# A hybrid attention and feed-forward kernel on one core: ScalarE's order written out in the gated stage, and VectorE's in the feed-forward stages

## The chip, the cores and the metric

The kernel runs on one core of a Trainium2 chip. The time is that of the device, in microseconds (us), for one execution. PE is TensorE (PEld its weight loads), ACT ScalarE, DVE VectorE, POOL GpSimd, SP SyncE, which issues the transfers.

## What is computed

x is 2 sequences of 1024 tokens by 512 columns. Four stages follow one another, each with a layernorm ahead of it and its result added to x: a gated linear recurrence, a feed-forward net, a causal two-map attention, and the feed-forward net again. The weights of the net are made ternary first. The two parts that the change touches:

```python
# gated stage, 16 heads of 32 columns
q, k, v, a, g = split(layernorm(x) @ w_in.T, 5)
q = q * rsqrt(mean(q * q over the head) + RMS_EPS)
a = clip(sigmoid(a + 2.0), 0.6, 0.9995);  u = tanh(k) * v
prefix = cumprod(a over a chunk of 64 tokens)
mem[t] = a[t] * mem[t - 1] + u[t] * min(prefix / 1e-6, 1)
y = (q * mem) * sigmoid(g) + (1 - sigmoid(g)) * v
x = x + y @ w_out.T
# feed-forward: w = ternary(w), scale per 64 columns from mean(abs(w))
h = silu(layernorm(x) @ w_gate.T) * (layernorm(x) @ w_up.T)
x = x + (h @ w_proj.T) * rsqrt(mean(h * h) + RMS_EPS)
```

## The kernel before, in words

x stays on the chip as 16 tiles of 128 tokens by 512 columns. The gated stage works on 4 blocks of 512 tokens. All its matmuls are plain f32 and give columns on the partitions and tokens along the row.

**Start of a block.** `Input` (L284) holds the layernorm of four x tiles: statistics on DVE (L109, L110), the root on ACT (`rstd`, L112), the reciprocal and the scaling `xn` on DVE (L128), four transposes on PE (`xnt_a`, L137) and a copy on ACT (`a_xt`, L313). For block 0 this goes tile by tile; for a later block the statistics are made at once by the constructor, at the end of the block before the previous one, `normal` scales two of the tiles in c = 0 and 1 and two in c = 2, and `turn` transposes two in c = 2 and two in c = 3.

**Queries.** `queries` (L322) projects q by chunks of 128 columns, copies it (L337), squares it (`sq`, L339) and sums the squares by head with a matmul each into `pss` (L329), 128 columns of `headmean` wide of which 16 are in use. The last of these matmuls, the root over 16 partitions and the reciprocal stand in `roots` and `factors` (L351 to L359); `rq_parts` keeps the factor in two parts, and `pr` (a matmul with `headrow`) spreads it over a chunk's columns.

**A block** runs over c = 0 to 3, chunks of 128 columns. PE: `project(kv[:, 0])` is k, `project(kv[:, 1])` is v, then come the transposes for the next block, group means of the ternary weights (`pm`), then `project(ag[:, 0])` and `project(ag[:, 1])`, 4 matmuls of 512 columns each (L317). kv and ag are tiles of two banks of psum, one bank for each half, from one pool of two buffers. After all four projections, the code emits on ACT u = tanh(k), v, a = sigmoid and gate (L461 to L468); then DVE and POOL make the recurrence by two scans and the row yt. **End of a block:** the next block's queries, then 16 matmuls `a_out` (L529) and the addition to x (L534); after the first of them `roots`, after the second `factors`.

**Ternary weights** (`Ternary`, 16 chunks of 128 by 1536): ACT makes mag and sign (L193, L195), PE the group mean `pm` of each third, ACT the copy `scale` (L203), DVE six steps (L209 to L218), which `step` deals out between the other work; the seventh stores the chunk, calls `begin` (mag and sign) of the next and loads the one three ahead.

**Feed-forward** (from L571): for each of 4 blocks, 16 values of f. `gate_up` (L616 to L631): 8 + 8 matmuls, silu on ACT, the product h on DVE (L622), a copy on ACT (L624), hs on DVE (L625), squares on ACT and their sum on POOL. `down` (L637) comes one f later on PE, into `f_out`. The next block's statistics are made at f = 6, its `normal` one f ahead of its transposes. In the last block of the first net, `beside` calls `normal_stats` at f = 2 and `normalise` at f = 4 to 11 for the attention's first sequence; `normalise` emits the scaling (`xn_b`, L128) and the transposes (`xnt_b`, L137) together, and it is called after `gate_up` and ahead of `down`.

**What sets the order.** A tile framework places the instructions. Where a stage holds `manual_schedule` for an engine, that engine runs them as the code emits them; otherwise a scheduler orders them. In the gated stage PE and DVE were by hand (ACT only for block 0's input, L403), in the feed-forward stages PE and ACT, in the attention PE. Waits are put in by the framework, tile by tile:

```python
fixed = {mybir.EngineType.PE, mybir.EngineType.DVE}
order.enter_context(tc.manual_schedule(engines=fixed))
```

Of the kernel before, what the change touches and what calls it, by code (L numbers as in the profile page):

```python
# [17 lines left out]
P = 128  # L18
# [24 lines left out]
def kernel(  # L43
# [58 lines left out]

    def layernorm_begin(tiles, name, norm=norm):

        n = len(tiles)
        mv = norm.tile([P, n, 2], F32, tag="ln_mv", name=f"mv_{name}")
        for j, i in enumerate(tiles):
            st = norm.tile([P, 6], F32, tag="ln_st", name=f"st_{name}_{j}")
            nc.vector.bn_stats(st, xres[i])  # L109
            nc.vector.bn_aggr(mv[:, j, :], st)  # L110
        rstd = norm.tile([P, n], F32, tag="ln_rstd", name=f"rstd_{name}")
        nc.scalar.activation(rstd, mv[:, :, 1], AF.Sqrt, bias=ln_eps)  # L112
        return mv, rstd
# [107 lines left out]
    with ExitStack() as s:  # L221
# [38 lines left out]
        headmean = wa.tile([P, NKC, P], F32, name="headmean")  # L260
        nc.gpsimd.memset(headmean, 0.0)
        heads = headmean[:, :, :16]
        nc.gpsimd.memset(heads, 1.0 / HD)
        for base, sign in ((0, 1), (HD - 1, -1)):
            nc.gpsimd.affine_select(
                out=heads, in_=heads, compare_op=ALU.is_ge, fill=0.0, base=base,
                pattern=[[sign * P, NKC], [-sign * HD, 16]], channel_multiplier=sign,
            )
# [3 lines left out]
        for base in (0, 32):  # L272
            nc.gpsimd.affine_select(
                out=headrow, in_=headrow, compare_op=ALU.not_equal, fill=1.0, base=base,
                pattern=[[4, NKC], [1, 4], [0, HD]], channel_multiplier=-1,
            )

        rq_parts = []
        for i in range(2):
            z = wa.tile([P, BLK], F32R, name=f"rq_parts{i}")  # L280
            nc.vector.memset(z.bitcast(F32), 0.0)
            rq_parts.append(z)

        a_start = []  # L284
        for i in range(2):
            z = wa.tile([P, BLK], F32, name=f"a_start{i}")
            nc.vector.memset(z, 0.0)
            a_start.append(z)

        class Input:  # L290


            def __init__(self, t, at_once=True):
                self.tiles = range(t * TPB, (t + 1) * TPB)
                self.stats = layernorm_stats(self.tiles, f"a{t}") if at_once else None
                self.xt = xt_pool.tile([P, NKC, BLK], F32, tag="xt", name=f"a_xt{t}")
                self.xn, self.one = {}, {}
# [23 lines left out]
        def queries(t, xt, begun=None):  # L321


            q = ap_.tile([P, NKC, BLK], F32, tag="q", name=f"q{t}")
            pss = bank(f"pss{t}")
            late = []

            def mean_square(c, sq):
                nc.tensor.matmul(  # L329
                    pss, headmean[:, c, :], sq, start=(c == 0), stop=(c == NKC - 1)  # L330
                )

            for c in range(NKC):
                pq = begun if begun and not c else bank(f"pq{t}_{c}")
                if pq is not begun:
                    project(pq, w_q, c, xt)
                nc.scalar.copy(q[:, c, :], pq)  # L337
                sq = ap_.tile([P, BLK], F32, tag="sq", name=f"sq{t}_{c}")
                nc.scalar.square(sq, pq)  # L339
                if late:  # L340
                    mean_square(*late.pop())
                late.append((c, sq))
                if c < 3 and t:
                    quantise(c)
                elif c and not t:
                    quantise(c - 1)
            parts = rq_parts[t % 2]

            rq = ap_.tile([16, BLK], F32, tag="rq", name=f"rq{t}", bufs=1)

            def roots():  # L351
                mean_square(*late.pop())
                nc.scalar.activation(rq, pss[:16, :], AF.Sqrt, bias=rms_eps[:16])

            def factors():
                nc.vector.reciprocal(rq, rq)
                hi, lo = parts[:16], parts[32:48]
                nc.vector.tensor_copy(hi, rq)
                nc.vector.tensor_sub(lo, rq, hi.bitcast(F32))  # L359

            return q, parts, roots, factors
# [27 lines left out]
        fixed = {mybir.EngineType.PE, mybir.EngineType.DVE}  # L389
        order.enter_context(tc.manual_schedule(engines=fixed))  # L390
        before = [None] * NKC
        first = Input(0, at_once=False)
# [10 lines left out]
        with tc.manual_schedule(engines={mybir.EngineType.Activation}):  # L403
            for j in range(TPB + 1):
                if j < TPB:
                    first.measure(j)
                if j:
                    first.normal(j - 1)
                    first.turn(j - 1)
                if j == 3:  # L410
                    begin(0, 0)
# [8 lines left out]
        following = Input(1)  # L420
        for t in range(NBLK):
            yt = wa.tile([P, NKC, BLK], F32, tag="yt", name=f"yt{t}")
            last = t == NBLK - 1
            for c in range(NKC):
# [9 lines left out]
                project(kv[:, 0, :], w_k, c, xt)  # L434
                if t + c == 0:
                    roots()
                    factors()
                project(kv[:, 1, :], w_v, c, xt)
                if t + c == 0:
                    quantise(3)  # L440
                    step()
# [26 lines left out]
                nc.scalar.activation(gate, ag[:, 1, :], AF.Sigmoid)  # L468
# [5 lines left out]
                start = a_start[c % 2]  # L474
# [13 lines left out]
                if not last and c < 2:  # L488
                    following.normal(c)
# [36 lines left out]
            for j, k in products:  # L526
                if k == 0:
                    po[j] = bank(f"a_out{t}_{j}")
                nc.tensor.matmul(  # L529
                    po[j], yt[:, k, ts(j, P)], w_out[:, k, :], start=(k == 0), stop=(k == NKC - 1)  # L530
                )
                if k == NKC - 1:
                    xi = xres[t * TPB + j]
                    nc.vector.tensor_add(xi, xi, po[j])  # L534
                    if not last:
                        if j == 0:
                            roots()
                        elif j == 1:
                            factors()
                        for i in ((), (), (3, 0), (1, 2, 3))[j]:  # L540
                            quantise(i)
                            step()
            if not last:
                q, rq = q_next, rq_next
                following = Input(t + 2) if t + 2 < NBLK else None
# [13 lines left out]

    def normal_stats(b):  # L560
        stats[b] = layernorm_stats(range(b * NQ, (b + 1) * NQ), f"b{b}")
        xts[b] = edge_sb.tile([P, NKC, SEQ], F32, tag="xt", name=f"b_xt{b}")
# [11 lines left out]
    def feed_forward(which, store, first, beside=None):  # L574


        with ExitStack() as s:
# [82 lines left out]
            for f in range(NF):  # L660
# [3 lines left out]
                tc.manual_schedule(engines={mybir.EngineType.PE, mybir.EngineType.Activation})  # L664
# [10 lines left out]
            for t in range(NBLK):  # L675
# [5 lines left out]
                for f in range(NF):  # L681
# [28 lines left out]
        {2: lambda: normal_stats(0)}  # L710
        | {f: lambda j=f - 4: normalise(0, j, edge_bank) for f in range(4, 4 + NQ)},
# [564 lines left out]
```

## Time and profile before

| what | us |
|---|---|
| three runs: lowest, median, highest | 2138.49, 2139.43, 2142.36 |
| the profiled execution's span | 2138.4 |
| gated stage, 0 to 403: PE busy, DVE, ACT | 378.3, 289.4, 162.8 |
| first feed-forward, 403 to 765: PE, DVE, ACT | 361.8, 132.4, 144.0 |
| attention, 765 to 1773: PE, DVE, ACT | 1004.6, 540.0, 390.5 |
| second feed-forward, 1773 to the end: PE, DVE, ACT | 358.8, 121.9, 137.6 |
| granted TensorE clock, by stage | 0.98, 1.00, 1.00, 0.99 |

The span runs from the first to the last instruction that the profiler saw. The runs' times take in the little that lies around it. A busy time is the sum of an engine's instructions; the granted clock is TensorE's, as a share of full speed. In a line of the timeline the first number is the start, the second the time from the first start to the last end of a group of like instructions, and what stands in brackets is the idle time ahead of it and whose end it waited for. In the table of waits the numbers are the sum of the idle time, the number of waits and the longest.

### The profile page before, as it was taken

To read this page: it belongs to the slowest core of one execution; us is meant where nothing else is said; L and a number is where in the kernel's file an instruction comes from. 1 tells how busy PE (TensorE), PEld (TensorE's weight loads), DVE (VectorE), ACT (ScalarE), POOL (GpSimd) and SP (SyncE) were. 2 spreads that over 40 slices of the span, in tenths; PEclk is the share of its full clock that TensorE was granted. 3 is DMA by queue.
4 is the path that set the end of the run, shared out by engine and by line. 5 is a ranking of instruction groups with operands and counts; after the bars stand their busy time and mean duration, and the time that the engine had idled before them with its cause. 6 is when DMAs were issued, how large, how long until landed. Compare 5 with 4: busy or idle time off the path is not lost.

```text
span 2138.4 us, 28060 instructions
## 1 busy us (share of the span) xinstructions
PE 2103.5 (98%) x10632; PEld 1245.7 (58%) x10632; DVE 1083.6 (51%) x2282; ACT 834.9 (39%) x1589; POOL 462.3 (22%) x808
## 2 busy tenths in 40 slices
PE   8999999999999999999999999999999999999998
PEld 4444444588888854444444444444444447888887
DVE  5766768643344234555555465364646672433322
ACT  5343434244344322444444422243434433343433
POOL 1413223122222221211212113021212231121222
PEclk9999999999999999999999999999999999999999
DMA  7121111600000111101010101111110033000000
GB/s 264 66 89 59 59 59 59 250 1 1 1 1 1 35 47 37 41 22 45 21 46 21 46 8 37 38 32 34 31 36 16 14 114 133 8 13 20 1 21 20
DMA packets 51000, 98.71 MB, mean 46 GB/s; under 512 B 10801, under 2 KB 19121, under 8 KB 50865
## 3 DMA queue, kind: packets, MB, share of 16 engines
q1 hardware_dynamic: 50864, 96.93, 13.9%
q8 instruction: 83, 1.36, 0.3%
q14 instruction: 53, 0.43, 0.1%
HBM read 58.75 MB, written 16.78 MB: 35 GB/s over the span
## 4 chain that ended last, share of the span: by engine, by line
PE 89%; DVE 7%; ACT 2%; POOL 1%; DMA 1%; issue 1%; SPq 0%; DVEq 0%; ACTq 0%; POOLq 0%
PE y L995 13%; PE g L616 11%; PE u L616 11%; PE f_out L637 11%; PE s L896 10%; PE pq L828 8%; PE t L957 8%; PE ag L317 3%; PE kv L317 3%; PE pv L793 3%; PE b_out L1064 2%; PE a_out L529 2%; PE mt L936 1%; POOL mem L502 1%; PE t L965 1%
## 5 line engine op out<-in xcount | busy, mean ns | idle before, releaser
L973 ACT ACTIVATE pr<-t 128x512 f32<-128x512 f32 (+3 forms) x768 | 314.8, 497 | 382.6 <-PE t L965 382.4
L906 DVE CUSTOM_DVE_ANT_0 s<-s,causal 128x128 f32<-128x128 f32 (+3 forms) x512 | 245.1, 510 | 124.9 <-PE s L896 116.2
L995 PE MATMUL y<-pr,val 128*64 128x512 f32 (+3 forms) x1536 | 292.1, 501 | 0.4 <-ACT ys L1012 0.2
L631 POOL TENSOR_TENSOR ssq<-ssq,sq 128x512 f32<-128x512 f32 x120 | 155.8, 1298 | 591.7 <-ACT sq L630 591.7
L622 DVE TENSOR_TENSOR h<-h,u 128x512 f32<-128x512 f32 x128 | 88.0, 687 | 351.3 <-PE u L616 345.7
L911 DVE TENSOR_REDUCE nmax<-s 128x1 f32<-128x512 f32 x256 | 164.9, 685 | 183.3 <-PE s L896 183.3
L616 PE MATMUL g<-xs,w 128*128 128x512 f32 x1024 | 257.7, 394 | 0.0
L637 PE MATMUL f_out<-w,hs 128*128 128x512 f32 x1024 | 254.3, 390 | 0.4 <-DVE hs L625 0.4
L616 PE MATMUL u<-xs,w 128*128 128x512 f32 x1024 | 253.2, 389 | 0.0
L896 PE MATMUL s<-gr,gr 32*128 32x512 f32 (+3 forms) x1536 | 250.6, 493 | 1.0 <-DVE nmax L906 0.9
L616 PEld LDWEIGHTS u<-xs,w 128*128 128x128 f32 x1024 | 192.2, 188 | 40.6
L637 PEld LDWEIGHTS f_out<-w,hs 128*128 128x128 f32 x1024 | 191.5, 188 | 40.7 <-DVE hs L625 1.1
L616 PEld LDWEIGHTS g<-xs,w 128*128 128x128 f32 x1024 | 190.0, 188 | 39.6 <-issue 1.0
L957 PE MATMUL t<-gr,gr 32*128 32x512 f32 (+3 forms) x1536 | 199.3, 534 | 0.0
L995 PEld LDWEIGHTS y<-pr,val 128*64 128x64 f32 x1536 | 93.5, 136 | 180.8 <-issue 105.8
L828 PE MATMUL pq<-b_xt,w_qk 128*128 128x512 f32 x384 | 176.1, 603 | 0.2 <-DVE x L654 0.2
L896 PEld LDWEIGHTS s<-gr,gr 32*128 32x128 f32 x1536 | 148.3, 185 | 46.7 <-issue 14.3
L976 POOL TENSOR_SCALAR_AFFINE_SELECT pr<-pr 128x256 f32<-128x256 f32 x256 | 102.0, 411 | 333.0 <-ACT pr L973 333.0
L624 ACT CAST hs<-h 128x512 fp32r<-128x512 f32 x128 | 79.4, 620 | 233.4 <-DVE h L622 233.4
L621 ACT ACTIVATE h<-g 128x512 f32<-128x512 f32 x128 | 76.5, 597 | 234.3 <-PE g L616 234.2
L625 DVE TENSOR_TENSOR hs<-h,hs 128x512 fp32r<-128x512 f32 x128 | 88.5, 691 | 83.1 <-ACT hs L624 83.1
L828 PEld LDWEIGHTS pq<-b_xt,w_qk 128*128 128x128 f32 x384 | 69.7, 189 | 88.3 <-issue 74.0
(160 smaller groups left out, 2249.7 us busy)
## 6 DMA issues: line engine op xcount, KB each, us to landing
w<-w_kept SPq DMA_DIRECT2D x32, 768.0 KB, 8.7
w_kept<-w SPq DMA_DIRECT2D x16, 768.0 KB, 3.2
gr<-gr SPq DMA_DIRECT2D x96, 128.0 KB, 2.3
w<-in_w_gu_dram SPq DMA_DIRECT2D x32, 256.0 KB, 2.9
share<-ys SPq DMA_DIRECT2D x128, 64.0 KB, 2.0
x<-in_x_dram SPq DMA_DIRECT2D x16, 256.0 KB, 6.8
w<-in_w_pt_dram SPq DMA_DIRECT2D x16, 256.0 KB, 3.7
w_qk<-in_wq_dram SPq DMA_DIRECT2D x8, 512.0 KB, 4.2
```

The lines of the kernel that those rows point to most:

```text
L317: nc.tensor.matmul(po, w[:, k, ts(c, P)], xt[:, k, :], start=(k == 0), stop=(k == NKC - 1))
L616: nc.tensor.matmul(po, ws[f][:, part, ts(k, P)], xs[:, e, k, :], start=(k == 0 and e == 0), stop=(k == NKC - 1 and e == 1),)
L631: nc.gpsimd.tensor_add(ssq, ssq, sq)
L637: nc.tensor.matmul(po[j], hp[:, e, ts(j, P)], ws[f][:, 2, :], start=(f == 0 and e == 0), stop=(f == NF - 1 and e == 1),)
L828: nc.tensor.matmul(po, w[:, k, ts(kind, P)], xts[b][:, k, ts(e, BLK)], start=(k == 0), stop=(k == NKC - 1),)
L896: nc.tensor.matmul(part, queries[:, ts(j, P)], keys[:, first : first + nk], start=True, stop=True,)
L906: nc.vector.tensor_tensor_reduce(part, part, causal[:, BLK - part.shape[-1] :], -1.0, 3.0e38, ALU.add, ALU.min, top,)
L911: nc.vector.tensor_reduce(top, part, AX.X, ALU.max, negate=True)
L957: nc.tensor.matmul(banks[u, e][:, :nq], keys[:, ts(kb, P)], queries[:, (qb + 1) * BLK - nq : (qb + 1) * BLK], start=True, stop=False,)
L973: nc.scalar.activation(pr[:, e, :nq], banks[u, e][:, :nq], AF.Exp)
L976: nc.gpsimd.affine_select(out=pr[:, :, :P], in_=pr[:, :, :P], compare_op=ALU.is_ge, fill=0.0, base=0, pattern=[[0, 2], [1, P]], channel_mu ...
L995: nc.tensor.matmul(y[64 * e : 64 * e + 64, lo:], all_values[:, HV * (NH * kb + h) : HV * (NH * kb + h) + 64], pr[:, e, : BLK - lo], start= ...
```

## The change

1. ACT goes by hand in the whole gated stage. u is emitted after the projection of k, v after that of v, a after that of a, gate after that of g.
2. A class `Measure` makes layernorm statistics in parts: the next-but-one block's in c = 2 of a block instead of after it, with its root on ACT beside that of `roots`; the next feed-forward block's at f = 2 to 5, one tile each, instead of all at f = 6; the attention's at f = 0 to 3 by pairs, with the root at f = 4, and `normalise` at f = 5 to 12. Block 3's root of the feed-forward statistics stands at c = 1 between the projections of k and v.
3. Four matmuls after the last query, each into 32 partitions of `pss` with a `headmean` 32 columns wide, give the mean squares of the queries; the squares are kept until then in four buffers. Root, reciprocal and parts go over 128 partitions, one factor of two parts in a tile by means of the masks `lower` and `in_low`, and `headrow` holds -1 and +1. One `a_start` takes the place of two.
4. Both feed-forward stages hold PE, DVE and ACT by hand.

The diff without its context; the building of the masks is cut.

```diff
@@ -102,13 +102,24 @@
+    class Measure:
...
+        def __init__(self, tiles, name, norm=norm):
+            self.tiles, self.name, self.norm, self.n = tiles, name, norm, len(tiles)
+            self.mv = norm.tile([P, self.n, 2], F32, tag="ln_mv", name=f"mv_{name}")
+        def some(self, js):
+            for j in js:
+                st = self.norm.tile([P, 6], F32, tag="ln_st", name=f"st_{self.name}_{j}")
+                nc.vector.bn_stats(st, xres[self.tiles[j]])
+                nc.vector.bn_aggr(self.mv[:, j, :], st)
+            return self
+        def root(self):
+            rstd = self.norm.tile([P, self.n], F32, tag="ln_rstd", name=f"rstd_{self.name}")
+            nc.scalar.activation(rstd, self.mv[:, :, 1], AF.Sqrt, bias=ln_eps)
+            return self.mv, rstd
...
+        return Measure(tiles, name, norm).some(range(len(tiles))).root()
@@ -259,31 +270,31 @@
-        headmean = wa.tile([P, NKC, P], F32, name="headmean")
...
+        headmean = wa.tile([P, 2, 16], F32, name="headmean")
+        nc.gpsimd.memset(headmean, 1.0 / HD)
...
+        for base, fill in ((0, -1.0), (HD // 2, 1.0)):
...
+        start = wa.tile([P, BLK], F32, name="a_start")
+        nc.vector.memset(start, 0.0)
@@ -292,5 +303,5 @@
-            def __init__(self, t, at_once=True):
+            def __init__(self, t, stats=None):
                 self.tiles = range(t * TPB, (t + 1) * TPB)
-                self.stats = layernorm_stats(self.tiles, f"a{t}") if at_once else None
+                self.stats = stats
@@ -324,9 +335,3 @@
-            pss = bank(f"pss{t}")
-            late = []
-            def mean_square(c, sq):
-                nc.tensor.matmul(
-                    pss, headmean[:, c, :], sq, start=(c == 0), stop=(c == NKC - 1)
-                )
+            squares = []
@@ -337,7 +342,5 @@
-                sq = ap_.tile([P, BLK], F32, tag="sq", name=f"sq{t}_{c}")
+                sq = ap_.tile([P, BLK], F32, tag="sq", name=f"sq{t}_{c}", bufs=NKC)
-                if late:
-                    mean_square(*late.pop())
-                late.append((c, sq))
+                squares.append(sq)
@@ -346,15 +349,22 @@
-            parts = rq_parts[t % 2]
+            parts = ap_.tile([P, BLK], F32R, tag="rq_parts", name=f"rq_parts{t}")
 
-            rq = ap_.tile([16, BLK], F32, tag="rq", name=f"rq{t}", bufs=1)
+            rq = ap_.tile([P, BLK], F32, tag="rq", name=f"rq{t}", bufs=1)
 
             def roots():
-                mean_square(*late.pop())
-                nc.scalar.activation(rq, pss[:16, :], AF.Sqrt, bias=rms_eps[:16])
+                pss = bank(f"pss{t}")
+                for c, sq in enumerate(squares):
+                    nc.tensor.matmul(
+                        pss[ts(c, HD)], headmean.rearrange("p a h -> p (a h)"), sq,
+                        start=True, stop=True,
+                    )
+                nc.scalar.activation(rq, pss, AF.Sqrt, bias=rms_eps)
 
             def factors():
                 nc.vector.reciprocal(rq, rq)
-                hi, lo = parts[:16], parts[32:48]
-                nc.vector.tensor_copy(hi, rq)
-                nc.vector.tensor_sub(lo, rq, hi.bitcast(F32))
+                nc.vector.tensor_copy(parts, rq)
+                nc.vector.scalar_tensor_tensor(
+                    parts, rq, in_low, parts.bitcast(F32), ALU.mult, ALU.subtract
+                )
 
@@ -388,6 +398,6 @@
-        fixed = {mybir.EngineType.PE, mybir.EngineType.DVE}
+        fixed = {mybir.EngineType.PE, mybir.EngineType.DVE, mybir.EngineType.Activation}
-        first = Input(0, at_once=False)
+        first = Input(0)
@@ -419,3 +428,3 @@
-        following = Input(1)
+        measured = Measure(range(TPB, 2 * TPB), "a1")
@@ -434,6 +443,18 @@
                 project(kv[:, 0, :], w_k, c, xt)
+                u = ap_.tile([P, BLK], F32, tag="u", name=f"u{n}")
                 if t + c == 0:
+                    measured.some(range(TPB))
                     roots()
                     factors()
+                    following = Input(1, layernorm_end(*measured.root()))
+                    nc.scalar.preload_act_table_set("sigmoid_and_others")
+                    following.normal(0)
+                    following.normal(1)
+                if last and c == 1:
+                    ff_stats = measured.root()
+                    nc.scalar.preload_act_table_set("sigmoid_and_others")
+                nc.scalar.activation(u, kv[:, 0, :], AF.Tanh)
                 project(kv[:, 1, :], w_v, c, xt)
+                v = ap_.tile([P, BLK], F32, tag="v", name=f"v{n}")
+                nc.scalar.copy(v, kv[:, 1, :])
@@ -453,2 +474,4 @@
                 project(ag[:, 0, :], w_a, c, xt)
+                a = ap_.tile([P, BLK], F32, tag="a", name=f"a{n}")
+                nc.scalar.activation(a, ag[:, 0, :], AF.Sigmoid, bias=two)
@@ -456,2 +479,4 @@
                 project(ag[:, 1, :], w_g, c, xt)
+                gate = ap_.tile([P, BLK], F32, tag="gate", name=f"gate{n}")
+                nc.scalar.activation(gate, ag[:, 1, :], AF.Sigmoid)
@@ -460,10 +485,2 @@
-                u = ap_.tile([P, BLK], F32, tag="u", name=f"u{n}")
-                nc.scalar.activation(u, kv[:, 0, :], AF.Tanh)
-                v = ap_.tile([P, BLK], F32, tag="v", name=f"v{n}")
-                nc.scalar.copy(v, kv[:, 1, :])
-                a = ap_.tile([P, BLK], F32, tag="a", name=f"a{n}")
-                nc.scalar.activation(a, ag[:, 0, :], AF.Sigmoid, bias=two)
-                gate = ap_.tile([P, BLK], F32, tag="gate", name=f"gate{n}")
-                nc.scalar.activation(gate, ag[:, 1, :], AF.Sigmoid)
@@ -487,3 +503,3 @@
                 nc.vector.tensor_mul(qn, pr, qn)
-                if not last and c < 2:
+                if 0 < t and not last and c < 2:
                     following.normal(c)
@@ -507,4 +523,7 @@
-                if last and c == 0:
-                    ff_stats = layernorm_begin(range(TPB), "f0_0")
+                if t + 2 < NBLK and c == 2:
+                    measured = Measure(range((t + 2) * TPB, (t + 3) * TPB), f"a{t + 2}")
+                    measured.some(range(TPB))
+                elif last and c == 0:
+                    measured = Measure(range(TPB), "f0_0").some(range(TPB))
@@ -537,4 +556,9 @@
                             roots()
+                            if t + 2 < NBLK:
+                                stats = measured.root()
+                            nc.scalar.preload_act_table_set("sigmoid_and_others")
                         elif j == 1:
                             factors()
+                            if t + 2 < NBLK:
+                                layernorm_end(*stats)
@@ -544,3 +568,3 @@
                 q, rq = q_next, rq_next
-                following = Input(t + 2) if t + 2 < NBLK else None
+                following = Input(t + 2, stats) if t + 2 < NBLK else None
@@ -559,6 +583,15 @@
-    def normal_stats(b):
-        stats[b] = layernorm_stats(range(b * NQ, (b + 1) * NQ), f"b{b}")
+    def begin_stats(b, js):
+        if b not in stats:
+            stats[b] = Measure(range(b * NQ, (b + 1) * NQ), f"b{b}")
+        stats[b].some(js)
+    def end_stats(b):
+        stats[b] = layernorm_end(*stats[b].root())
+    def normal_stats(b):
+        begin_stats(b, range(NQ))
+        end_stats(b)
@@ -663,3 +696,3 @@
             s.enter_context(
-                tc.manual_schedule(engines={mybir.EngineType.PE, mybir.EngineType.Activation})
+                tc.manual_schedule(engines=fixed)
@@ -688,3 +721,8 @@
-                    if t + 1 < NBLK and -2 <= j < TPB:
+                    if t + 1 < NBLK and -6 <= j < TPB:
+                        if j == -6:
+                            tiles = range((t + 1) * TPB, (t + 2) * TPB)
+                            measured = Measure(tiles, f"f{which}_{t + 1}", fp)
+                        if j < -2:
+                            measured.some([j + 6])
                         if j == -2:
@@ -692,6 +730,4 @@
                             place = (edge_sb, "xt") if t % 2 else (xsp, "xs")
-                            tiles = range((t + 1) * TPB, (t + 2) * TPB)
-                            measured = layernorm_stats(tiles, f"f{which}_{t + 1}", fp)
-                            following = FeedForwardInput(which, t + 1, *place, measured)
+                            stats = layernorm_end(*measured.root())
+                            following = FeedForwardInput(which, t + 1, *place, stats)
@@ -709,4 +745,5 @@
         0, False, ff_first,
-        {2: lambda: normal_stats(0)}
-        | {f: lambda j=f - 4: normalise(0, j, edge_bank) for f in range(4, 4 + NQ)},
+        {f: lambda f=f: begin_stats(0, range(2 * f, 2 * f + 2)) for f in range(NQ // 2)}
+        | {NQ // 2: lambda: end_stats(0)}
+        | {f: lambda j=f - 5: normalise(0, j, edge_bank) for f in range(5, 5 + NQ)},
```

More of the change, by code (lines that the diff above doesn't have):

```diff
@@ L101 @@
     norm = ctx.enter_context(tc.tile_pool(name="norm", bufs=2, reuse_waits="tile"))
-    def layernorm_begin(tiles, name, norm=norm):
[L105 to L113, printed above, removed]
+    class Measure:
[12 more added lines that the diff above has]
+            return self.mv, rstd
+    def layernorm_begin(tiles, name, norm=norm):
+        return Measure(tiles, name, norm).some(range(len(tiles))).root()
     def layernorm_end(mv, rstd):
@@ L257 @@
         chunk.append(Ternary(tp, 2, range(3)))
-        headmean = wa.tile([P, NKC, P], F32, name="headmean")
-        nc.gpsimd.memset(headmean, 0.0)
-        heads = headmean[:, :, :16]
-        nc.gpsimd.memset(heads, 1.0 / HD)
+        headmean = wa.tile([P, 2, 16], F32, name="headmean")
+        nc.gpsimd.memset(headmean, 1.0 / HD)
         for base, sign in ((0, 1), (HD - 1, -1)):
             nc.gpsimd.affine_select(
-                out=heads, in_=heads, compare_op=ALU.is_ge, fill=0.0, base=base,
-                pattern=[[sign * P, NKC], [-sign * HD, 16]], channel_multiplier=sign,
-            )
+                out=headmean, in_=headmean, compare_op=ALU.is_ge, fill=0.0, base=base,
+                pattern=[[0, 2], [-sign * HD, 16]], channel_multiplier=sign,
+            )
@@ new lines @@
+        lower = wa.tile([P, NKC], F32, name="lower")
+        nc.gpsimd.memset(lower, 1.0)
+        for base, sign in ((-HD // 2, 1), (HD - 1, -1)):
+            nc.gpsimd.affine_select(
+                out=lower, in_=lower, compare_op=ALU.is_ge, fill=0.0, base=base,
+                pattern=[[-sign * HD, NKC]], channel_multiplier=sign,
+            )
+        in_low = wa.tile([P, 1], F32, name="in_low")
+        nc.gpsimd.tensor_add(lower[:, :2], lower[:, :2], lower[:, 2:])
+        nc.gpsimd.tensor_add(in_low, lower[:, :1], lower[:, 1:2])
@@ L270 @@
         headrow = wa.tile([P, NKC, P], F32R, name="headrow")
         nc.gpsimd.memset(headrow.bitcast(F32), 0.0)
-        for base in (0, 32):
+        for base, fill in ((0, -1.0), (HD // 2, 1.0)):
             nc.gpsimd.affine_select(
-                out=headrow, in_=headrow, compare_op=ALU.not_equal, fill=1.0, base=base,
-                pattern=[[4, NKC], [1, 4], [0, HD]], channel_multiplier=-1,
-            )
[L278 to L288, printed above, removed]
+                out=headrow, in_=headrow, compare_op=ALU.not_equal, fill=fill, base=base,
+                pattern=[[HD, NKC], [1, 4], [0, HD]], channel_multiplier=-1,
+            )
+        start = wa.tile([P, BLK], F32, name="a_start")
+        nc.vector.memset(start, 0.0)
         class Input:
-            def __init__(self, t, at_once=True):
+            def __init__(self, t, stats=None):
@@ L346, in queries @@
                     quantise(c - 1)
-            parts = rq_parts[t % 2]
-            rq = ap_.tile([16, BLK], F32, tag="rq", name=f"rq{t}", bufs=1)
+            parts = ap_.tile([P, BLK], F32R, tag="rq_parts", name=f"rq_parts{t}")
+            rq = ap_.tile([P, BLK], F32, tag="rq", name=f"rq{t}", bufs=1)
             def roots():
-                mean_square(*late.pop())
-                nc.scalar.activation(rq, pss[:16, :], AF.Sqrt, bias=rms_eps[:16])
+                pss = bank(f"pss{t}")
[5 more added lines that the diff above has]
+                nc.scalar.activation(rq, pss, AF.Sqrt, bias=rms_eps)
             def factors():
                 nc.vector.reciprocal(rq, rq)
-                hi, lo = parts[:16], parts[32:48]
-                nc.vector.tensor_copy(hi, rq)
-                nc.vector.tensor_sub(lo, rq, hi.bitcast(F32))
+                nc.vector.tensor_copy(parts, rq)
+                nc.vector.scalar_tensor_tensor(
+                    parts, rq, in_low, parts.bitcast(F32), ALU.mult, ALU.subtract
+                )
             return q, parts, roots, factors
@@ L401, in begin @@
             )
[L403 to L411, printed above, removed]
+        for j in range(TPB + 1):
+            if j < TPB:
+                first.measure(j)
+            if j:
+                first.normal(j - 1)
+                first.turn(j - 1)
+            if j == 3:
+                begin(0, 0)
         for k in range(1, NKC):
@@ L472 @@
                 nc.vector.tensor_scalar(a, a, A_MIN, A_MAX, ALU.max, ALU.min)
-                start = a_start[c % 2]
                 nc.vector.tensor_copy(start[:, 0:BLK:CHUNK], a[:, 0:BLK:CHUNK])
@@ L558 @@
     stats, xts = {}, {}
+    def begin_stats(b, js):
[4 more added lines that the diff above has]
+        stats[b] = layernorm_end(*stats[b].root())
+        xts[b] = edge_sb.tile([P, NKC, SEQ], F32, tag="xt", name=f"b_xt{b}")
     def normal_stats(b):
-        stats[b] = layernorm_stats(range(b * NQ, (b + 1) * NQ), f"b{b}")
-        xts[b] = edge_sb.tile([P, NKC, SEQ], F32, tag="xt", name=f"b_xt{b}")
+        begin_stats(b, range(NQ))
+        end_stats(b)
     def normalise(b, j, psum):
```

## The prediction

> **What bounds it now.** I read the page's busy times and its granted clock first, then TensorE's (PE's) waits in total, then the timeline of each engine in the gated stage (0 to 403 us) and in the last block of the first FFN.
>
> ```profile
> PE 2103.5 (98%) x10632; PEld 1245.7 (58%) x10632; DVE 1083.6 (51%) x2282; ACT 834.9 (39%) x1589; POOL 462.3 (22%) x808
> ```
> ```profile
> PE xnt_a L137 <- DVE xn_a L128: 11.5, 4, 6.1
> PE pss L329 <- ACT sq L339: 7.0, 3, 2.4
> PE ag L317 <- ACT gate L468: 2.9, 2, 2.8
> PE a_out L529 <- DVE q L487: 2.6, 1, 2.6
> ```
>
> PE is the bound: it idles 35 us, some 23 of them in the gated stage. So a step helps only if it shortens PE's own stream or one of these waits, and any wait put into PE's stream is paid in full. PE's timeline gives the prices:
>
> ```profile
> 72.05 8.60 PE L317 MATMUL ag<-a_xt,w_in 128*128 128x512 f32 x16
> 88.89 7.03 PE L317 MATMUL ag<-a_xt,w_in 128*128 128x512 f32 x16
> 114.56 1.12 PE L329 MATMUL pss<-sq,headmean 128*128 128x512 f32 x2 [2.32 <-ACT sq L339]
> 208.30 2.08 PE L329 MATMUL pss<-sq,headmean 128*128 128x512 f32 x2 [2.38 <-ACT sq L339]
> 787.01 1.93 PE L810 MATMUL pl<-b_xt,w_l 128*32 128x256 f32 x32
> ```
>
> Two projections run 16 instructions in 7.03 us, 0.43 each; after a 3.94 us gap the same took 8.60, at a granted clock of 0.50. **The clock's price** is thus about 1.7 us after a long gap. Gaps of 2.31, 2.38 and 2.76 us cost it too; 2.32, 2.61 and 1.16 did not. I take 1.7 from 3 us up, and 1.0 on average for 2.3 to 2.8.
>
> **Taken away, gated stage.** (1) Query mean squares: 8 instructions of 512 columns a block, 8 x 0.43 = 3.43 us. The nearest row is pl, also in four 32-column tiles: 32 instructions of 256 columns would take 32 x 0.214 = 6.83 us in series and took 1.86 to the next start, 3.7 times as fast. So 0.95 us; bounds 0.86 (perfect overlap) and 3.43 (none). Gain 4 x 2.48 = 9.9. (2) Waits with their slow clock, as each piece's length less its matmuls: block 0, c=2 (xn late) 5.85; the square behind mag and sign on ACT at the three block ends 2.6, 4.3 and 4.15; block 2, c=1 0.4; block 3, c=2 (gate behind the rstd) 4.75; block 3's end 3.9. Together 26.0. All removed: 35.9.
>
> **Added, gated stage.** Today u, v, a and gate are emitted after both halves of kv and ag. The change emits u between project(kv[:,0]) and project(kv[:,1]), and a between the halves of ag. The two halves are one tile, and in the program as built the first matmul of each second half waits for the ACT instruction that has just read the first half: 32 new waits in PE's stream, with nothing behind them on PE that may pass. One costs: PE's tail 0.17 (3.60 shown for a 3.43 stream), 0.03 to ACT's start (24.31 to 24.34), tanh 0.60 or sigmoid 0.69, 0.05 back (114.51 to 114.56), 0.10 restart (1.12 against 1.02). That is 0.95 for u, 1.04 for a. Short gaps; no clock price by the 1.16 row. Eleven plain u: 10.5; fifteen plain a: 15.6, and 0.2 for the last, which lies beside two transposes.
>
> The other u stand behind something on ACT's fixed order, and PE now waits for that too:
> - Block starts 1 to 3: u follows mag and sign of the next chunk, which wait for DVE to finish the chunk before last.
> ```profile
> 133.53 1.48 ACT L193 ACTIVATE mag<-w 128x1536 bf16<-128x1536 f32 x1 [1.71 <-DVE scale L216]
> 136.32 1.48 ACT L195 ACTIVATE sign<-w 128x1536 bf16<-128x1536 f32 x1 [1.30 <-DVE w L218]
> ```
> a_out began at 115.52, so sign ends 22.3 later, 22.55 with the added reciprocal; u ends at 23.1 and PE goes on at 23.25. Project k ends 18.75 after a_out's start (15.32 + 3.43): 4.5 us each, 13.4 in all, and 3 x 1.7 of clock. Before, u was as late, but no matmul waited for it.
> - Block 0, c=0: v waits for pss, root 0.68, second root 0.30, table load 1.28 and tanh: 3.25. Then pm waits for v's copy and mag (1.48), which the scheduler had put early: 2.25. Clock 2.0 for both.
> - Block 3, c=1: the root of the FFN statistics stands ahead of u, and waits for DVE to end all of c=0.
> ```profile
> 358.42 0.18 DVE L110 BATCH_NORM_AGGREGATE mv_f<-st_f 128x2 f32<-128x6 f32 x1
> ```
> ```profile
> 358.64 0.30 ACT L112 ACTIVATE rstd_f<-mv_f,ln_eps 128x4 f32<-128x4 f32 x1 [5.33 <-DVE mv_f L110]
> ```
> Today this is 52.7 us after block 2's a_out. In the changed order a comes at 33.0; DVE's chain from there is c=0 and its chunk to 51.2, statistics to 54.4, root 54.8, table load 56.1, tanh 56.7: PE goes on at 56.85 where k ended at 40.45, so 16.4 us, and 1.7 of clock. DVE has caught up by the end: yt 3 at 110.8, its products from 113.9, so nothing more there.
>
> Added: 10.5 + 15.8 + 13.4 + 5.1 + 5.5 + 2.0 + 16.4 + 1.7 = 70.4. **Gated stage: 70.4 - 35.9 = +34.5 us.**
>
> **FFN.** DVE's order becomes the emitted one. Statistics in four pieces and normal one f ahead lie beside 5.4 us of matmuls per f, with DVE at 2.3 us: nothing, and nothing to win, since PE idles 0.0 us between 420 and 760. But normalise() in the first FFN's last block emits an x's scaling and its transposes together, after h and hs. Today the scaling goes before its f:
>
> ```profile
> 697.03 0.60 PE L137 MATMUL xnt_b<-ident,xn_b 128*128 128x128 f32 x4
> ```
> ```profile
> 697.30 0.69 DVE L622 TENSOR_TENSOR h<-h,u 128x512 f32<-128x512 f32 x1 [3.29 <-PE u L616]
> 697.91 0.54 DVE L128 TENSOR_SCALAR xn_b<-x,mv_b,rstd_b 128x512 f32<-128x512 f32 x1
> 698.68 0.69 DVE L625 TENSOR_TENSOR hs<-h,hs 128x512 fp32r<-128x512 f32 x1 [0.23 <-ACT hs L624]
> ```
>
> The xn_b shown here is for the next f. In the changed order it follows hs: 698.68 + 0.60 + 0.55 + 0.05 = 699.88, plus 0.10 restart, and xnt_b, ahead of f_out on PE, moves from 697.03 to there: 2.95 us, eight times, 23.6. The gap shown is 2.7 us, so 8 x 1.0 of clock. **FFN: +31.6 us** (bounds 23.6, no slow clock, and 37.2).
>
> **At nothing:** root, reciprocal and parts on 128 instead of 16 partitions (DVE's 16x512 subtract takes 0.68, its 128x512 add 0.69); five more small GpSimd instructions and fewer memsets at the start, beside the x loads; fewer table loads, on an ACT 39% busy. SP's queue keeps its order, and weight loads have landed when mag asks. If a chunk's load were late, u would carry it to PE; it isn't, as chunks are loaded three ahead. The second FFN and attention keep PE's order.
>
> **Sum.** +34.5 + 31.6 = +66. Span 2138.4 becomes 2204.5; 1.0 us lies around it (median of the runs 2139.43): **2205.5 us**, 3.1% more. A difference under 0.2% can't be told from none.
>
> [...]
>
> **Rivals.**
> - *The hand order wins.* Only what is removed counts, 35.9: 2103.5 us. It decides if the second halves needn't wait for ACT and the FFN's transposes still find xn ready, so that all added waits stay under 36 us. For it: these waits are in today's profile. Against it: the waits in the built program and the rows above. 0.04; all but a quarter of it, where the sums nearly cancel, faster.
> - *The tiles don't overlap* (the change isn't what it says): 3.43 stays, +10: 2215. The pl row speaks against. 0.09.
> - *DVE reaches block 3's statistics early*, and u waits 1 us: 18 - 1 = 17 less, 2188. Against it: DVE was busy without a break from 341 to 377. 0.07.
> - *The clock stays down* at the plain waits as well: 26 x 1.7 = 44 more, 2250. Against it: the 1.16 row. 0.08.
> - The forecast: 0.72. With no slow clock at all it is 2205.5 - 8.8 - 8 = 2189; with it at every gap over 2 us and 0.2 more a plain wait, 2218.
>
> Range 2185 to 2228: it takes in the forecast's bounds, the serial tiles and the early statistics. Chances: faster 0.03, within 0.2% 0.01, slower 0.96.
>
> **What will show it.** PE waits "kv <- ACT u" and "ag <- ACT a", some 0.7 us each, sixteen and fifteen times; three kv waits near 4.3 and one near 16; eight "xnt_b <- DVE xn_b" of 2.7; pss as 8 instructions in about 1 us. No wait xn_a, sq or gate left. I am wrong if the kv and ag waits are missing, or if ag's 16 instructions stay at 7.03 us of start to end.

## The result, and the profile after

The changed kernel takes 2219.86 us (median of four runs, 2216.36 to 2223.92) against 2139.18 before: 1.0375 of the time, interval 1.0361 to 1.039. That is 80.7 us slower; 66 were forecast, and 2219.86 lies within the stated range. The profiled execution took 2216.36 us with a span of 2214.7, so the median run lies 3.5 above the profiled one, which no step of the prediction covers. The four runs go with TensorE's granted clock: spans of 2214.7, 2217.0, 2219.2 and 2222.2 us at 0.982, 0.982, 0.981 and 0.979. The profiled run is the fastest of them.

The page of the changed kernel, first its busy times. PE has 12.8 us more busy time, though no matmul was added; the rest of the 76.3 us by which the span grew, 63.5, is idle time of PE:

```profile
PE 2116.3 (96%) x10623; PEld 1249.6 (56%) x10632; DVE 1096.0 (49%) x2279; ACT 827.0 (37%) x1581; POOL 461.2 (21%) x812
```

PE's waits in total (us, times, longest). The waits of before on sq, gate and q are gone; four new ones stand in their place, where the prediction put them. Of the waits on xn_a the one of 3.94 in block 0 is gone; what is left is the kernel's start, which before had as well:

```profile
PE kv L328 <- ACT u L456: 37.5, 16, 14.5
PE xnt_b L148 <- DVE xn_b L139: 30.6, 8, 3.9
PE ag L328 <- ACT a L476: 11.7, 15, 0.8
PE xnt_a L148 <- DVE xn_a L139: 6.8, 3, 6.1
PE pm L214 <- ACT mag L204: 2.1, 1, 2.1
```

PE's timeline in the gated stage: a plain chunk of columns in block 0, the mean squares at block 0's end, the start of block 1, and block 3's c = 1:

```profile
47.68 3.60 PE L328 MATMUL kv<-a_xt,w_in_qk 128*128 128x512 f32 x8
51.96 3.70 PE L328 MATMUL kv<-a_xt,w_in 128*128 128x512 f32 x8 [0.69 <-ACT u L456]
55.50 0.59 PE L214 MATMUL pm<-mag,groupmean 128*128 128x512 bf16 x2
55.93 3.60 PE L328 MATMUL ag<-a_xt,w_in 128*128 128x512 f32 x8
60.31 3.70 PE L328 MATMUL ag<-a_xt,w_in 128*128 128x512 f32 x8 [0.78 <-ACT a L476]
...
116.58 1.07 PE L357 MATMUL pss<-sq,headmean 128*32 128x512 f32 x8
117.57 7.13 PE L548 MATMUL a_out<-w_out,yt 128*128 128x512 f32 x16
...
128.63 3.60 PE L328 MATMUL kv<-a_xt,w_in_qk 128*128 128x512 f32 x8
136.32 5.40 PE L328 MATMUL kv<-a_xt,w_in 128*128 128x512 f32 x8 [4.10 <-ACT u L456]
...
355.07 3.59 PE L328 MATMUL kv<-a_xt,w_in_qk 128*128 128x512 f32 x8
373.20 5.29 PE L328 MATMUL kv<-a_xt,w_in 128*128 128x512 f32 x8 [14.53 <-ACT u L456]
```

From 47.68 to 51.96 is 4.28 us for a stream of 3.43: the wait for u costs 0.85 there, and 0.11 more until the next instruction (3.54 for 3.43), so 0.27 beside the gap of 0.69. The wait for a costs 0.95 up to 60.31. The eight mean-square instructions take 0.99 to the next start. At block 1's start v comes 7.69 after k, and at block 3's c = 1 18.13. ACT shows why u is late there. At block 1 it stands behind sign, which waits for DVE; at block 3 it stands behind the root, which waits for DVE's statistics, and behind a table load:

```profile
134.30 1.48 ACT L206 ACTIVATE sign<-w 128x1536 bf16<-128x1536 f32 x1 [1.31 <-DVE w L229]
135.69 0.58 ACT L456 ACTIVATE u<-kv 128x512 f32<-128x512 f32 x1
...
370.94 0.30 ACT L119 ACTIVATE rstd_f<-mv_f,ln_eps 128x4 f32<-128x4 f32 x1 [10.98 <-DVE mv_f L114]
371.25 1.28 ACT L455 ACT_TABLE_LOAD   x1
372.55 0.60 ACT L456 ACTIVATE u<-kv 128x512 f32<-128x512 f32 x1
```

In the last block of the first feed-forward net, PE, and below it DVE and POOL, in one value of f:

```profile
743.20 1.98 PE L649 MATMUL u<-xs,w 128*128 128x512 f32 x8
748.98 1.09 PE L148 MATMUL xnt_b<-ident,xn_b 128*128 128x128 f32 x4 [3.81 <-DVE xn_b L139]
749.72 3.10 PE L670 MATMUL f_out<-w,hs 128*128 128x512 f32 x8
```
```profile
745.28 0.69 DVE L655 TENSOR_TENSOR h<-h,u 128x512 f32<-128x512 f32 x1 [8.64 <-PE u L649]
746.65 0.69 DVE L658 TENSOR_TENSOR hs<-h,hs 128x512 fp32r<-128x512 f32 x1 [0.68 <-ACT hs L657]
747.26 1.58 DVE L139 TENSOR_SCALAR xn_b<-x,mv_b,rstd_b 128x512 f32<-128x512 f32 x1
```
```profile
747.29 1.26 POOL L664 TENSOR_TENSOR ssq<-ssq,sq 128x512 f32<-128x512 f32 x1 [10.94 <-ACT sq L663]
```

The order h, hs, xn_b is the forecast one. But xn_b, 0.54 us before, takes 1.58 here, beside an addition of POOL's that starts 0.03 after it. The gap is 3.81 instead of the forecast 2.7, and over the eight values of f the f_out behind it runs 3.10 to 3.76 instead of 2.1.

### The profile page after: what moved, and what is told of

Same layout as the page of the kernel before. It is cut to its first block, busy times and chain, and to the rows that moved or that the text cites. A ratio compares the mean times of both kernels' runs of the same rounds, so it can differ in the third digit from the quotient of the medians.

```text
span 2214.7 us, 28070 instructions
## 1 busy us (share of the span) xinstructions
PE 2116.3 (96%) x10623; PEld 1249.6 (56%) x10632; DVE 1096.0 (49%) x2279; ACT 827.0 (37%) x1581; POOL 461.2 (21%) x812
## 4 chain that ended last, share of the span: by engine, by line
PE 92%; DVE 4%; ACT 2%; issue 1%; DMA 1%; SPq 0%; POOL 0%; DVEq 0%; ACTq 0%; POOLq 0%
PE y L1032 12%; PE f_out L670 11%; PE g L649 10%; PE u L649 10%; PE s L933 10%; PE pq L865 8%; PE t L994 8%; PE ag L328 5%; PE kv L328 5%; PE pv L830 3%; PE b_out L1101 2%; PE pq L328 2%; PE a_out L548 2%; PE mt L973 1%; PE t L1002 1%
## 5 line engine op out<-in xcount | busy, mean ns | idle before, releaser
L670 PE MATMUL f_out<-w,hs 128*128 128x512 f32 x1024 | 265.2, 403 | 0.4 <-DVE hs L658 0.4
L670 PEld LDWEIGHTS f_out<-w,hs 128*128 128x128 f32 x1024 | 199.4, 196 | 42.9 <-DVE hs L658 1.1
L328 PE MATMUL ag<-a_xt,w_in 128*128 128x512 f32 x256 | 116.7, 599 | 11.9 <-ACT a L476 11.7
```

The source lines that it names most:

```text
L328: nc.tensor.matmul(po, w[:, k, ts(c, P)], xt[:, k, :], start=(k == 0), stop=(k == NKC - 1))
L670: nc.tensor.matmul(po[j], hp[:, e, ts(j, P)], ws[f][:, 2, :], start=(f == 0 and e == 0), stop=(f == NF - 1 and e == 1),)
```

## The experiments

Each time stands beside runs of the kernel before on the same chip (medians 2139.3 to 2140.1). "Less" is against the changed kernel's median of 2219.86 where nothing else is said. Its four runs spread over 7.6 us, so such a difference is good to a few us; where it matters the profiles' times of single stages stand beside it.

**e_split: the halves in tiles of their own.**

```diff
-                kv, ag = big(f"kv{n}"), big(f"ag{n}")
+                pk, pv, pa, pg = (big(f"{i}{n}") for i in ("pk", "pv", "pa", "pg"))
```

(`big` then hands out one bank, from four buffers; each half's uses follow.)

> The changed kernel with four one-bank psum tiles (pk, pv, pa, pg) in place of kv and ag with two halves each; same psum, same order on every engine. Theory (the half-tile waits): the plain u and a waits of 0.69 to 0.78 us go, 9 x 0.97 + 12 x 1.07 in blocks 0 to 2, the two long ones at the starts of blocks 1 and 2 with their slow clock (6.1 and 6.8), and 3.1 in block 0, c = 0: 37.5 us. Block 3: u of c = 1 still stands behind the statistics' root and now holds up the next k, which takes that bank, and VectorE's chain paces the block, so 8 to 27 us go there. In all 45 to 64 us less: 2156 to 2175 us, no wait kv or ag on ACT except near block 3's c = 2. Rival (ScalarE or VectorE is late anyway and the waits come back as others): above 2200.

2162.56 us (ratio 1.0104, 1.0089 to 1.012): 57.3 less than the changed kernel. In the profile the gated stage ends at 378.22 us, against 433.31 in the changed kernel and 403.08 before. PE's waits in total: all 31 on u and a are gone, and one new wait for u stands at block 3's c = 2, where the expectation had it:

```profile
PE xnt_b L148 <- DVE xn_b L139: 30.6, 8, 3.9
PE xnt_a L148 <- DVE xn_a L139: 7.0, 3, 6.2
PE pk L328 <- ACT u L456: 5.5, 1, 5.5
```

On PE, ACT and DVE the order is the same, by hand in both (on POOL two neighbouring instructions change places once); what changed is what a wait is attached to. So the gated stage's loss needs the sharing of a tile by a matmul and the ACT instruction ahead of it, and the rival, ACT or DVE late anyway, falls, but for the 5.5 us in block 3. For the five long waits the sharing is one of two conditions: ACT is late there as well, and e_root and e_mag take four of them away with the tiles left as they are.

**e_hoist: xn_b one f ahead.**

```diff
+        xn = ahead.pop(i, None) or normal(i, j, stats[b], f"b{i}")
+        pt = transposed(xn, f"b{i}", psum)
...
+    def beside_0(j):
+        normalise(0, j, edge_bank)
+        if j + 1 < NQ:
+            scale_ahead(0, j + 1)
```

(`scale_ahead` puts the scaled tile into `ahead`; the first is made with `end_stats`.)

> The changed kernel, with each xn_b of the first FFN's last block scaled one f earlier, behind that f's hs, instead of straight ahead of its transposes. Theory (xn stands behind h and hs): the eight waits xnt_b <- xn_b of 3.8 us and their slow clock go, 47.7 us less: 2172 us, the first FFN back at 362.7 us; xn_b still takes near 1.58 us, hidden. Rival (VectorE's order by hand in the FFN, or the statistics in pieces, cost the time by themselves): 2205 or more.

2170.53 us (1.0146, 1.0131 to 1.0161): 49.3 less. PE and DVE in one f:

```profile
739.41 1.98 PE L665 MATMUL u<-xs,w 128*128 128x512 f32 x8
741.23 0.60 PE L148 MATMUL xnt_b<-ident,xn_b 128*128 128x128 f32 x4
741.58 2.11 PE L686 MATMUL f_out<-w,hs 128*128 128x512 f32 x8
```
```profile
743.48 1.61 DVE L139 TENSOR_SCALAR xn_b<-x,mv_b,rstd_b 128x512 f32<-128x512 f32 x1
```

The transposes follow u at once. xn_b is as slow as in the changed kernel, but an f early and so hidden. The first FFN (feed-forward net) takes 362.65 us, 362.67 before: DVE's order by hand and the statistics in pieces cost nothing by themselves.

**e_both: these two, and the root behind the gate.**

```diff
-                if last and c == 1:
-                    ff_stats = measured.root()
-                    nc.scalar.preload_act_table_set("sigmoid_and_others")
                 nc.scalar.activation(u, pk, AF.Tanh)
...
                 nc.scalar.activation(gate, pg, AF.Sigmoid)
+                if last and c == 1:
+                    ff_stats = measured.root()
+                    nc.scalar.preload_act_table_set("sigmoid_and_others")
```

> The changed kernel with both of these edits, and with block 3's root of the FFN statistics on ScalarE behind the gate of c = 1 instead of ahead of its u. Theory: every added wait goes and what was to be removed stays removed (35.9 us by the prediction), except that VectorE's chain of block 3 may hold a_out by some us: 2139 - 36 + 0 to 8 = 2103 to 2111 us, below the kernel before. Rival (the hand order on ScalarE loses by itself): 2135 or more.

2108.5 us (0.9853, 0.9839 to 0.9868): faster than both kernels, 30.8 under the one before. PE's largest waits:

```profile
PE xnt_a L148 <- DVE xn_a L139: 7.2, 3, 5.9
PE pm L214 <- ACT mag L204: 2.1, 1, 2.1
PE b_out L1117 <- POOL share L1104: 1.1, 1, 1.1
PE pr L501 <- DVE xs L176: 1.1, 1, 1.1
```

The rival, that an order by hand on ACT loses, falls: most of the forecast gain is there (30.8 of 35.9) once nothing waits on half a tile, xn_b is an f ahead and the root is out of u's way. DVE holds up block 3 by 1.8 us (1.10, 0.48 and 0.19).

**e_noport: the eight additions of ssq on DVE, behind xn_b.**

```diff
-                    nc.gpsimd.tensor_add(ssq, ssq, sq)
+                    if which or t < NBLK - 1 or f not in beside:
+                        nc.gpsimd.tensor_add(ssq, ssq, sq)
+                    else:
+                        later.append(sq)
...
                         beside[f]()
+                        if later:
+                            nc.vector.tensor_add(ssq, ssq, later.pop())
```

> The changed kernel, with the eight additions of ssq that run beside an xn_b on VectorE behind xn_b instead of on GpSimd. xn_b took 1.58 us in the changed kernel and 0.54 before. Theory (it is held up by GpSimd's addition that runs at the same time): xn_b takes 0.54 again, the gap ahead of xnt_b falls from 3.81 to 2.77: 8.3 us less, 2211.5, if the slow clock costs 2.2 us a gap as after 3.81; down to 2194 if a gap of 2.77 costs none. Rival (xn_b is long for another reason, such as what it reads): it stays at 1.58 and the time at 2219 or more.

2208.06 us (1.0321, 1.0303 to 1.0338): 11.8 less. DVE, and PE, in one f:

```profile
750.38 0.54 DVE L139 TENSOR_SCALAR xn_b<-x,mv_b,rstd_b 128x512 f32<-128x512 f32 x1
750.84 0.69 DVE L722 TENSOR_TENSOR ssq<-ssq,sq 128x512 f32<-128x512 f32 x1
```
```profile
751.07 1.05 PE L148 MATMUL xnt_b<-ident,xn_b 128*128 128x128 f32 x4 [2.77 <-DVE xn_b L139]
751.77 3.36 PE L673 MATMUL f_out<-w,hs 128*128 128x512 f32 x8
```

Without POOL beside it xn_b takes 0.54 in the same place, and the gap is 2.77, as the prediction had it (2.7). So POOL's addition is what holds xn_b up, for 1.04 us. One f takes 10.48 (xnt_b at 751.07 and 761.55), 4.54 more than before's 5.94: the slow clock (granted at 0.57 from 751 to 755) costs 1.6 beyond the 2.95 of the stall; from 751.07 on an f takes 10.27 to 10.48, which makes it 1.4 to 1.6. The first FFN is 12.0 us shorter than in the changed kernel (398.3 and 410.3), 8.0 of it by shorter waits (22.6 and 30.6) and the rest by the clock. In these two profiles the spans are only 8.6 apart, since e_noport's gated stage, with the same code, ended 4.5 later.

**e_root: the root behind the gate, alone,** on the changed kernel, with the edit shown at e_both.

> The changed kernel with block 3's root of the FFN statistics emitted on ScalarE behind the gate of c = 1 instead of ahead of its u. Theory (u stands behind a root that VectorE has not reached): the wait of 14.5 us and its slow clock, 16.4 us together, become one plain wait of 0.95: 15.4 less, 2204.5 us. Rival (VectorE is late in block 3 in any case and a_out waits for it): less than 6 us gained, 2214 or more.

2204.08 us (1.0303, 1.0286 to 1.032): 15.8 less, 15.4 expected. PE's wait for u, 37.5 us in the changed kernel, with a longest of 14.5:

```profile
PE kv L328 <- ACT u L453: 23.8, 16, 4.1
```

**e_mag: mag and sign behind the next block's first u.**

```diff
+                        if j == TPB - 1:
+                            hold.append(t)
...
                 nc.scalar.activation(u, kv[:, 0, :], AF.Tanh)
+                if hold:
+                    hold.clear()
+                    chunk[0].begin()
```

(`step` doesn't begin a chunk while `hold` is filled.)

> The changed kernel with mag and sign of the chunk that the last step of a block begins emitted on ScalarE behind the next block's first u instead of ahead of it. Theory (u waits behind sign, sign for VectorE): the three block starts lose 4.1 us of wait each and their slow clock (6.1, 6.8 and 6.2 less a plain wait of 0.95 each): 16.2 less, 2203.7 us. Rival (mag comes too late for the group mean behind v, which then waits as long): 2215 or more.

2203.36 us (1.03, 1.0285 to 1.0316): 16.5 less, 16.2 expected. PE at block 1's start, to be read against 128.63, 136.32 and its 4.10 above. The rival's wait of pm for mag isn't there:

```profile
128.51 3.60 PE L328 MATMUL kv<-a_xt,w_in_qk 128*128 128x512 f32 x8
132.85 3.70 PE L328 MATMUL kv<-a_xt,w_in 128*128 128x512 f32 x8 [0.75 <-ACT u L456]
136.39 0.38 PE L214 MATMUL pm<-mag,groupmean 128*128 128x512 bf16 x1
```

**b_ffn: the kernel before, with VectorE by hand in the feed-forward stages as its only edit.**

```diff
-                tc.manual_schedule(engines={mybir.EngineType.PE, mybir.EngineType.Activation})
+                tc.manual_schedule(engines=fixed | {mybir.EngineType.Activation})
```

> The kernel before with one edit: both feed-forward stages hold VectorE by hand as well; statistics and normalise stay where they were. Theory (xn_b stands behind h and hs once VectorE runs as emitted): eight waits xnt_b <- xn_b of 3.8 us and 2.2 of slow clock come back, as in the changed kernel, 48 more: 2187 us; the eight statistics at once at f = 2 may add up to 5. Rival (the loss belongs to the statistics in pieces or to normalise's later place): 2145 or less.

2185.17 us (1.0217, 1.0202 to 1.0232): 45.1 slower than before, by that line alone. PE's waits:

```profile
PE xnt_b L137 <- DVE xn_b L128: 30.6, 8, 4.0
...
PE u L616 <- ACT h L621: 2.2, 1, 2.2
```

The first is the changed kernel's wait to the tenth. The second, at f = 4 (694.23), is the price of eight statistics at once, emitted at f = 2 under a fixed order: DVE works on them from 685.0 to 694.2, and h of f = 3 stands behind them. The changed kernel, with its statistics in pieces, doesn't have it. The first FFN takes 413.1 us, 50.5 more than before; the gated stage ends 3.4 earlier (399.69), where the wait of 2.6 for q is gone.

**b_pss: the kernel before, with the mean squares of the change alone** (part 3 of the change).

> The kernel before with the third part of the change alone: four 32-column matmuls after the queries, squares kept in four buffers, root and factors over 128 partitions, one a_start. Theory: 8 instructions in 1.0 us instead of 3.43, four times 2.4 = 9.7 less, and the three waits pss <- sq of 2.3 us with their slow clock (11 in all) go as well, since the squares are now wanted 3.4 us later: 2119 us. Rival (the squares are late anyway, and pss waits behind the first a_out): 2129 us.

2122.3 us (0.9921, 0.9906 to 0.9935): 17.8 less than before, between the two, nearer the theory's 2119 than the rival's 2129. Of PE's waits pss <- sq 0.2 is left of 7.0. But the reason that the theory gives, that the squares are wanted later, is not separated from another: ACT's order is the scheduler's here, and at each of these block ends it now puts sign behind the third square, for which PE had waited, instead of ahead of it. At the end of block 0 the eight instructions stand right behind the first a_out, but take 1.70 to the next start instead of 1.0:

```profile
109.03 3.60 PE L531 MATMUL a_out<-w_out,yt 128*128 128x512 f32 x8
112.55 1.77 PE L349 MATMUL pss<-sq,headmean 128*32 128x512 f32 x8
114.25 7.13 PE L531 MATMUL a_out<-w_out,yt 128*128 128x512 f32 x16
```

At the other two block ends they take 2.25 and 1.71, so 2.7 of the 3.3 us that are missing lie here. It is the rival's point in small: the last square, behind sign, is late at all three, and the weight load (PEld) ahead of its matmuls waits.

```profile
PEld pss L349 <- ACT sq L336: 2.3, 3, 1.1
```

**e_best: the three repairs, and block 0's first group means later.**

```diff
-                        pieces = ((0, 1), (2,), (3,))
+                        pieces = ((), (0, 1, 2), (3,)) if c == 0 else ((0, 1), (2,), (3,))
```

> The version with all three repairs (separate tiles, xn_b one f ahead, the root behind the gate), and the group means of block 0's c = 0 moved behind the second ag projection, since pm waited 2.06 us for mag there with 1.7 of slow clock behind it. Theory (nothing else waits for that group mean): 3.8 less than with the three repairs alone (2108.5): 2104.7 us. Rival (the scale copies come late and VectorE's steps with them, or the mean waits at its new place): 2108 or more.

2105.45 us (0.9843, 0.983 to 0.9857). The wait pm <- mag is gone from PE's list, and the span is 5.1 shorter than e_both's. Of that 1.2 is an earlier start (block 0's first k at 26.43 and 27.67), so 3.9 are left where 3.8 were expected; by the runs' intervals the two versions can't be told apart. It has the lowest median here, 34 us under the kernel before.

## Why the prediction was right, and where it was short

Direction, mechanism and place were right; the sum was short by 10 us of span. That small a miss is in part luck: the first FFN was short by 16.1, and 5.9 of that is hidden by the gated stage, where 4.3 too much was forecast, and by what follows. The median of 2219.86 lies above the forecast's own upper figure of 2218; that it is within the range of 2185 to 2228 is owed to the room left for serial tiles, which didn't come.

| step | predicted | measured |
|---|---|---|
| eleven plain waits for u | 10.5 | 10.8 |
| the waits for a | 15.8 | 15.8 |
| three block starts, with clock | 18.5 | 18.9 |
| block 0, c = 0, with clock | 7.5 | 5.3 |
| block 3, c = 1, with clock | 18.1 | 16.4 |
| taken away | -35.9 | -37.0 |
| gated stage | +34.5 | +30.2 |
| first FFN | +31.6 | +47.7 |
| all that follows | 0 | -1.6 |
| span | +66.1 | +76.3 |

The gated stage is measured at the first g (403.08 before, 433.31 after), the FFN from there to the first b matmul (765.75 and 843.64). The plain waits are the sums of the list of waits, less the five long ones for u (7.8 and 11.7 us are left), plus 0.27 each for tail and restart. Block 0, c = 0 is v's lateness of 3.0 us and the group mean's of 2.3. "Taken away" is what is left of the gated stage's +30.2, not a measurement of its own, and it holds up to 2 us of luck at the start: block 0's first k comes at 25.62 here, and at 25.5 to 27.7 in the experiments on this kernel. e_both agrees with it: its gated stage is 28.2 shorter than before's, with some 5.5 of waits and slow clock left in it and a start 2.0 later.

- **The half-tile waits** are as forecast in number, place and size; e_split removes them. The prices came from single rows (3.60 for a stream of 3.43, 0.60 for tanh), and each stands in the sum eleven or fifteen times, so an error of 0.1 in both would have made 2.6 us.
- **The long waits** were worked out by following ACT's order back to DVE's chain: 4.5 forecast and 4.2 to 4.3 found at a block start, 16.4 and 14.7 at block 3, where DVE came to the statistics 1.4 earlier than forecast (367.62, which is 49.8 after a_out's start and not 51.2). e_mag and e_root remove each by itself. The granted clock behind the wait at block 1's start was 0.68 (136.3 to 141.6), and behind block 3's 0.69 (373.2 to 378.4).
- **Block 0, c = 0** carried 2.0 for a clock price that isn't in this profile: after gaps of 2.93 and 2.06 the matmuls ran at 3.70 and 3.60. That too is luck. e_hoist and e_noport have the same code up to there and the same gap of 2.93, and their v took 5.37 and 5.21. The changed kernel's line, and below it e_hoist's:

```profile
33.14 3.70 PE L328 MATMUL kv<-a_xt,w_in 128*128 128x512 f32 x8 [2.93 <-ACT u L456]
...
34.14 5.37 PE L328 MATMUL kv<-a_xt,w_in 128*128 128x512 f32 x8 [2.93 <-ACT u L456]
```

- **The term that failed in size** is the FFN's "2.95 us, eight times" and "8 x 1.0 of clock". On the mean an f took 11.95 (11.3 and 12.5 by turns) instead of 5.94, which is 6.01 more and not 3.95. Of the 2.06 that were missing, 1.04 is xn_b's length: the prediction moved a row of 0.54 to a new place and didn't ask who else runs there. In the old place POOL was idle (from 718.41 to 723.06, around an xn_b at 721.64); in the new one it adds ssq, as e_noport shows. The other 1.0 is the clock (granted at 0.53 from 736.7 to 742.0 and 0.67 from 748.9 to 753.5): 2.0 a gap at 3.81 us, and 1.4 to 1.6 still at e_noport's 2.77, where 1.0 was taken. The upper bound of 37.2 for the FFN was 10.5 too low.
- **The mean squares** in column tiles take 0.99 us to the next start, 0.95 forecast; the rival of serial tiles is out.
- **The other rivals.** That the hand order wins was false of this kernel; it does win with three repairs: e_both, with other tiles, xn_b an f ahead and the root behind the gate, gives 2108.5, where that rival had 2103.5. "DVE reaches block 3's statistics early" is out by the 14.53 us. "The clock stays down" at the plain waits is out as well: no group of matmuls behind a plain wait took longer than 3.70 us, and over 81 us with six plain waits the granted clock (column after the busy times) was 1.00, against 0.53 in 5 us behind the first xnt_b gap (3.94).

```profile
47.70:128.60 80.90, 76.39 (x198) 33.50 (x199) 56.96 (x69) 33.98 (x48) 26.41 (x15) 1.00 0.20 68
...
736.70:742.00 5.30, 5.22 (x15) 4.33 (x16) 0.00 (x0) 0.59 (x1) 0.00 (x0) 0.53 0.00 0
```

- **Slips in the readings**, none of which carries the sum: the granted clock over the 8.60 us after the gap of 3.94 is 0.82, and 0.50 holds for 72 to 74 us only; PE idles 24.7 us in the gated stage (403 less 378.3) and not some 23; and DVE wasn't busy without a break from 341 to 377, it waits 1.15 twice for POOL's mem. And 32 x 0.214 is 6.85.

## What to carry to other kernels

When an order is written out by hand, read which tile each wait is attached to: here an early reader of one half of a tile stopped the writer of the other half, 31 times. In the kernel before the code had the reader behind both halves, so that no matmul waited for it. A step that a scheduler had pulled ahead (xn_b by one f) must be pulled ahead in the code before the engine is fixed, since a fixed engine runs what the code says. And a duration taken from a row holds for the neighbours it had there (xn_b took 0.54 us in its old place and 1.58 in the new one); look at what the other engines do at the new place.

## What the runs showed of the hardware

- A 128x512 f32 TENSOR_SCALAR on DVE, xn_b, took 0.54 us with POOL idle (the kernel before, e_noport) and 1.57 to 1.61 when POOL's TENSOR_TENSOR of 1.26 to 1.29 us started 0.03 us after it (the changed kernel, e_hoist). Of the two it is xn_b that is held up: it ends 0.29 us behind POOL's addition (748.84 and 748.55), which took 1.26 beside it and no longer than without it (1.29). By the profile xn_b starts 0.03 earlier, and yet it is the one that takes longer. By what means the addition holds it up, no run shows.
- The length of a gap alone doesn't decide the slow clock. The gap of 2.93 in block 0 left v at 3.70 us in the changed kernel, e_root and e_mag, and at 5.37 and 5.21 in e_hoist and e_noport, with the same code up to there. The wait of 2.06 us for mag left the clock at 1.00 in the changed kernel (38.9 to 43.0) and at 0.70 in e_both (37.9 to 43.6, the projection 5.29 instead of 3.60), which has no gap of 2.93 ahead of it. What decides it is not shown. The gap of 2.06 in e_both cost 1.7 us and those of 2.77 in e_noport 1.4 to 1.6 each, where the prediction took 1.0 for gaps of 2.3 to 2.8.
